# First chunk of a Mamba layer: order of loads, norms, bias sums and row fetches

## Chip, cores, metric

One core of one Trainium2 chip. The metric is device time in microseconds, the median of several executions. The kernel before was run three times: 5859.45, 5865.35 and 5869.25 us.

## The reference

The input is x, (4, 384, 64, 64) in float32. Two layers follow each other, each added to its input after a group norm. The first is a Mamba block over the 4096 tokens of each image; the second is a windowed attention with convolved values (outlook), which the change does not touch. The Mamba block, cut:

```python
xn = layernorm(group_norm(x)) * ln_w + ln_b              # per token, 384 channels
xb, z = split(xn @ in_proj_w.T)                          # 768 channels each
xc = silu(causal_conv4(xb) + conv_b)
dt, Bm, Cm = split(xc @ x_proj_w.T)                      # 24, 16, 16
dt = softplus(dt @ dt_w.T + dt_b)
h = exp(dt * A) * h + (dt * xc) * Bm                     # per channel 16 states, over the tokens
y = (h . Cm + xc * D) * silu(z)
out = y @ out_proj_w.T
```

## The kernel before, in words

Each image is cut along its tokens into 17 chunks of 241, so there are 68 chunks. A chunk goes through a front (norm, projections, convolution, dt, B and C), a scan and an end (gate, output projection). The scan of a chunk is cut into 12 units: a unit has two groups of 32 channels with 16 states, held as 128 partitions by eight rows of 242 in a tile h. For a unit, POOL and DVE multiply the rows of dt*x (dxr) with B into h (s_inputs, line 747, and s_inputs2, line 762), ACT makes the decays da = exp(dt*A) in eight activations (s_decay, 771), DVE scans twice (s_scan, 783), POOL multiplies h with C (s_outputs, 793) and PE sums over the states (s_sum, 798).

The rows of dt and dt*x must lie four times over the partitions. So the front stores dt (f_log, 477) and dt*x (f_dtx, 509) to DRAM, tensors dtd and dxd, with four DMAs for each store, and SP reads them back for two units at a time, again in four DMAs each: s_fetch (731) reads dxr from dxd, s_fetch_dt (740) reads dtr from dtd. f_xd (444) and f_spread (483) do the same for B and C through bcd.

Nothing is scheduled by a planner. Each engine runs what the program issues, in the order in which it issues it (class InOrder, whose line 53 is why all instructions stand under L53 in the profile; they are told apart by the names of their tiles). The tool that builds the program adds semaphore waits by the tiles that an instruction reads and writes, and reuses buffers by pool: the pool pmm has two PSUM buffers for nearly all matmul results of the front. All DMAs here are issued by SP, over eight semaphores in turn, so a DMA also waits for the eighth before it.

In the steady state a loop over steps s (line 949) issues the parts of up to six chunks by a written plan (line 605), with the scan of unit s, the inputs of units s + 1 and s + 2, and the outputs of unit s - 1. Ahead of it a straight piece of code (lines 886 to 946), the head, brings the first chunk to the end of its front and the second chunk to the end of its norm. In the loop's first steps the second chunk's projection (f_x, 358) is issued at step -1, and the rest of its front is caught up (catch_up, 677).

The head's steps that the change moves: loads (213 to 231 and f_load, 281); group-norm coefficients of the image (x_coeffs, 184); the norm over channels in seven parts (f_mean, f_center, f_square, f_var, f_root, f_pow, f_scale, lines 289 to 333), which run on PE, DVE, ACT, PE, ACT, ACT, DVE in that order; w_bias (247), which multiplies the projection's weights by the norm's bias in one-column matmuls into the tile pw, six blocks for each half of the weights' columns; w_scale (258), which copies those sums to bxz and scales the weights win by the norm's weight; w_taps (235), which writes the convolution's diagonal matrices cdiag on POOL; f_conv (379), f_silu (410), f_bc (434, tile ps_xd), f_dt (454, ps_dt), f_plog (504, ps_lg), f_z (400, tile zs).

Of the kernel before, what the change touches and what calls it, by code (L numbers as in the profile page):

```python
# [7 lines left out]
F32 = mybir.dt.float32  # L8
# [4 lines left out]
P = 128  # L13
C = 384
NCB = C // P
# [95 lines left out]
def mamba_layer(ctx, tc, x, w, x1, sc1, bi1, bi4, consts, early, behind):  # L111
# [40 lines left out]
    def load(name, shape, pool=wp):  # L152
        t = pool.tile(shape, F32, tag=name, name=name)
        sp.dma_start(t, w[name])
        return t
# [58 lines left out]
    for i in range(NCB * NX):  # L214
        x_stat(0, i, x_load(0, i))

    lnw = load("lnw", [P, NCB], wf)
    lnb = load("lnb", [P, NCB], wf)
    win = wf.tile([P, NCB, 2 * DI], F32, tag="win", name="win")
    sp.dma_start(win[:, :, :DI], w["win"][:, :, :DI])  # L220
    cw = load("cw", [P, NJ, KC], wf)
    cbias = load("cbias", [P, NJ], wf)
    wx = load("wx", [P, NJ, P], wf)
# [23 lines left out]
    def w_bias(j0, j1):  # L247
        for j in range(j0, j1):
            for cb in range(NCB):
                pe.matmul(  # L250
                    pw[:, j : j + 1],
                    win[:, cb, j * P : (j + 1) * P],
                    lnb[:, cb : cb + 1],
                    start=(cb == 0),
                    stop=(cb == NCB - 1),
                )

    def w_scale(half):
        js = slice(NJ * half, NJ * (half + 1))
        ve.tensor_copy(bxz[:, js], pw[:, js])  # L260
        for cb in range(NCB):
            part = win[:, cb, DI * half : DI * (half + 1)]
            ve.tensor_scalar(part, part, lnw[:, cb : cb + 1], None, ALU.mult)
# [17 lines left out]
    def f_load(c):  # L281
        c.xt = iof.tile([P, NCB, XT], F32, tag="xt", name="xt")
        sp.dma_start(
            c.xt[:, :, : c.n], x[c.b, :, c.t0 : c.t0 + c.n].rearrange("(p cb) l -> p cb l", cb=NCB)
        )
        if c.n < TM:
            gp.memset(c.xt[:, :, c.n : TM], 0.0)

    def f_mean(c):
        t = c.t  # L290
        c.sc, avs, c.bias = coeffs[c.b]
        c.ps = pmm.tile([P, 2, TM], F32, tag="mm", name="ps_ln")
        for cb in range(NCB):
            pe.matmul(c.ps[:, 0, :t], avs, c.xt[:, cb, :t], start=(cb == 0), stop=(cb == NCB - 1))

    def f_center(c, u=None):

        t = c.t
        c.u = front.tile([P, NCB, TM], F32, tag="u", name="u") if u is None else u
        ve.scalar_tensor_tensor(  # L300
            c.u[:, :, :t],
            c.xt[:, :, :t],
            c.sc,
            c.ps[:, 0:1, :t].to_broadcast([P, NCB, t]),
            ALU.mult,
            ALU.subtract,
        )

    def f_square(c, room=None):
        t, u = c.t, c.u  # L310
        if room is None and c is live.get(2):
            room = xo.rearrange("p cb r w -> p cb (r w)")[:, :, 2 * XT :]
        if room is None:
            room = front.tile([P, NJ, KC - 1 + TM], F32, tag="xb", name="sq")
        c.sq = room[:, :NCB, :TM]
        ae.activation(c.sq[:, :, :t], u[:, :, :t], AF.Square, bias=c.bias)

    def f_var(c):

        t = c.t  # L320
        c.ps = pmm.tile([P, 2, TM], F32, tag="mm", name="ps_var")
        for cb in range(NCB):
            pe.matmul(c.ps[:, 0, :t], avg, c.sq[:, cb, :t], start=(cb == 0), stop=(cb == NCB - 1))

    def f_root(c):
        v = c.ps[:, 0, : c.t]
        ae.activation(v, v, AF.Ln, bias=eps)

    def f_pow(c):
        v = c.ps[:, 0, : c.t]  # L330
        ae.activation(v, v, AF.Exp, scale=-0.5)
# [26 lines left out]
    def f_x(c, jj):  # L358
        t = c.t
        if jj == 0:  # L360
            c.xb = front.tile([P, NJ, KC - 1 + TM], F32, tag="xb", name="xb")
            if c.t0 == 0:
                ae.copy(c.xb[:, :, 0 : KC - 1], pad.unsqueeze(2).to_broadcast([P, NJ, KC - 1]))
            else:
                ae.copy(c.xb[:, :, 0 : KC - 1], halo[c.b])
        pp = project(c, jj)
        ae.copy(c.xb[:, 2 * jj : 2 * jj + 2, KC - 1 : KC - 1 + t], pp[:, :, :t])
        if jj == NJ // 2 - 1 and c.t0 + c.n < L:
            halo[c.b] = small.tile([P, NJ, KC - 1], F32, tag="halo", name="halo")
            ae.copy(halo[c.b], c.xb[:, :, t : t + KC - 1])  # L370
# [8 lines left out]
    def f_conv(c, jj):  # L379
        t = c.t  # L380
        if jj == 0:
            c.xc = []
        c.xc.append(cross.tile([P, 2, 1 + TM], F32, tag=f"xc{jj}", name="xc"))
        c.cv = pp = pmm.tile([P, 2, TM], F32, tag="mm", name="ps_cv")
        for h in range(2):
            j = 2 * jj + h
            for k in range(KC):
                pe.matmul(
                    pp[:, h, :t], cdiag[:, j, k, :], c.xb[:, j, k : k + t], start=(k == 0), stop=(k == KC - 1)
                )  # L390
        if jj < NJ // 2 - 1:
            conv_out(c, jj, AF.Identity)
        first_column(c, c.xc[jj], c.last.xc[jj] if c.ci else None)
# [491 lines left out]

    first, second, third = chunk(0), chunk(1), chunk(2)
    spare = xo.rearrange("p cb r w -> p cb (r w)")
    f_load(first)
    f_load(second)
    sp.dma_start(win[:, :, DI:], w["win"][:, :, DI:])  # L890
    ssum = load("ssum", [P, CG])
# [4 lines left out]
        norm_part(norms[0][1])  # L896
    w_taps(0, 2)
    f_mean(first)
    w_bias(0, 2)
    f_center(first)  # L900
    f_load(third)
    f_square(first)
    f_var(first)
    w_bias(2, 3)
    f_root(first)
    f_pow(first)
    w_bias(3, NJ)
    f_scale(first)
    w_scale(0)
    ve.tensor_scalar_mul(pad, bxz[:, :NJ], -1.0)  # L910
    w_taps(2, NJ)
    f_x(first, 0)
    f_mean(second)
    ve.reduce_sum(cws, cw, AX.X)
    ve.tensor_mul(cws, cws, bxz[:, :NJ])
    ve.tensor_add(cbias, cbias, cws)
    f_center(second, spare[:, :, :TM])
    f_x(first, 1)
    f_square(second, spare[:, :, XT:])
    f_conv(first, 0)  # L920
    f_var(second)
    f_root(second)
    f_pow(second)
    f_x(first, 2)
    f_scale(second)
    f_conv(first, 1)
    f_conv(first, 2)
    f_silu(first)
    w_bias(NJ, 2 * NJ)
    w_scale(1)  # L930
    f_bc(first)
    f_xd(first)
    f_spread(first)
    for jj in range(NJ // 2):
        f_dt(first, jj)
    f_b(first)
    for jj in range(NJ // 2):
        f_plog(first, jj)
        f_dtx(first, jj)
    f_log(first)  # L940
    ae.activation(aneg, aneg, AF.Exp)
    ve.tensor_scalar_mul(aneg, aneg, -1.0)
    for j in range(NJ):
        gp.tensor_scalar(ddiag[:, j, :], ident, dvec[:, j : j + 1], None, ALU.mult)
    for jj in range(NJ // 2):
# [2 lines left out]
    front_end = NU * (len(chunks) - 1) - 1  # L948
    for s in range(-4, NU * (len(chunks) + 2)):
        k, m = divmod(s, NU)  # L950
        if m % 2 == 0 and unit(s + 4) is not None:
            s_fetch(s + 4)
        if m % 2 == 0 and unit(s + 2) is not None:
            s_fetch_dt(s + 2)
        parts(s, EARLY)
        if m % 4 == 3 or s >= NU * len(chunks):
            norm_part(False)

        if (u := unit(s + 1)) is not None:
            s_inputs2(u)  # L960
        if (u := unit(s - 3)) is not None and not u.first and u.j % 2:
            s_gate(u)
        parts(s, READY)

        b, ci = chunks[k][:2] if 0 <= k < len(chunks) else (B, 0)
        if b + 1 < B:
            n, e = divmod(NU * ci + m - 3, NU // 2)
            if e == 0 and 0 < n <= NCB * NX:
                x_stat(b + 1, n - 1, pending.pop())
            if e == 1 and 0 <= n < NCB * NX:  # L970
                pending.append(x_load(b + 1, n))
            if e == 2 and n == NCB * NX:
                x_coeffs(b + 1)
        for i in range(2):
            if (u := unit(s)) is not None:
                s_scan(u, i)
            if i == 1:
                parts(s, SCAN)
            if (u := unit(s + 1)) is not None:
                if i == 0:  # L980
                    s_carry(u)
                s_decay(u, i)
            if i == 0 and (u := unit(s - 1)) is not None:
                s_save(u)
        if (u := unit(s - 1)) is not None:
            s_outputs(u)
        norm_part(True)
        parts(s, POOL)
        if (u := unit(s + 2)) is not None:
            s_inputs(u)  # L990
        if (u := unit(s - 2)) is not None and not u.first:
            s_sum(unit(s - 3), u)
        parts(s, MID)
        parts(s, LATE)
        if s == front_end:
            fronts.close()
        if s >= front_end:
            over = das[0] if s >= NU * len(chunks) - 1 else None
            behind(lambda: pmm.tile([P, 2, TM], F32, tag="mm", name="psv").rearrange("p a b -> p (a b)"), over)
# [592 lines left out]
```

## Time and profile before

| what | us |
|---|---|
| median of three executions | 5865.35 |
| profiled execution, its own time | 5861.92 |
| its span, first to last instruction | 5860.1 |
| busy: POOL, PE, DVE, ACT | 5392.2, 5295.0, 5241.6, 4848.9 |
| first projection of the first chunk starts (PE) | 45.54 |
| first store of dt*x is issued (SP) | 82.92 |
| first decay starts (ACT) | 101.48 |
| first scan starts (DVE) | 103.19 |
| first outputs of POOL start | 107.57 |

Times in the timeline are from the start of the span. A row of it merges equal instructions that follow each other: start, length of the whole row, engine, operation, written tile and read tiles, count; the bracket tells how long the engine was idle before the row and what ended that. A float32 matmul is shown as two passes, each with its weight load (PEld), so x12 is six matmuls. SPq is SP's queue of DMA issues; the row's length is that of issuing, not of landing.

### The profile page before, as it was taken

The page shows a single profiled execution, that of the slowest core. Times are in us where ns is not written, and L with a number is a line of the kernel's source. Part 1 is how long each engine was busy: PE and PEld are TensorE (multiplying, and loading weights), DVE is VectorE, ACT ScalarE, POOL GpSimd, SP SyncE. Part 2 cuts the span into 40 slices and gives each one's busy share as a digit, 9 for nine tenths or more (in the row PEclk, how much of TensorE's full clock was granted, in tenths as well). Part 3 has the DMA queues.
Part 4 walks back from the last instruction along what each step waited for, and adds up shares of the span by engine and source line. Part 5 has one row for each costly group of instructions (what it writes and reads, how often), then busy time and mean ns, then how long its engine had stood idle before and what let it go on. Part 6 is the DMA issues. An engine that isn't in the chain of part 4 may idle for free.

```text
span 5860.1 us, 126156 instructions
## 1 busy us (share of the span) xinstructions
PE 5295.0 (90%) x46114; PEld 3820.7 (65%) x46114; DVE 5241.6 (89%) x4269; ACT 4848.9 (83%) x13283; POOL 5392.2 (92%) x2045
## 2 busy tenths in 40 slices
PE   6888888888999999998999999999999995899999
PEld 5666666666666666666666666666666663666555
DVE  4999999999999999999999999999999997787444
ACT  4888888888888888888898888889889885677665
POOL 3999999999999999999999999999999998899433
PEclk9999999999999999999999999999999997999999
DMA  4555554445666666666666666656666655666444
GB/s 133 145 142 143 143 144 134 131 131 139 166 169 174 171 179 162 173 171 159 176 177 174 179 168 171 170 148 173 170 167 169 162 152 158 199 211 206 159 168 154
DMA packets 758875, 955.11 MB, mean 163 GB/s; under 512 B 211488, under 2 KB 660972, under 8 KB 758124
## 3 DMA queue, kind: packets, MB, share of 16 engines
q1 hardware_dynamic: 758252, 947.04, 58.7%
q8 instruction: 362, 5.93, 0.4%
q14 instruction: 261, 2.14, 0.1%
HBM read 720.92 MB, written 225.70 MB: 162 GB/s over the span
## 4 chain that ended last, share of the span: by engine, by line
ACT 36%; PE 25%; DVE 17%; DMA 5%; POOL 5%; SPq 4%; issue 4%; DVEq 0%; ACTq 0%; POOLq 0%
ACT da L53 20%; DVE h L53 14%; PE ps_in L53 4%; SPq L53 4%; POOL h L53 4%; PE ps_v L53 4%; PE y L53 3%; PE psv L53 3%; ACT L53 3%; PE ps_cv L53 2%; PE ps L53 2%; ACT zs L53 2%; PE pso L53 2%; ACT xc L53 2%; PE psa L53 2%
## 5 line engine op out<-in xcount | busy, mean ns | idle before, releaser
L53 DVE TENSOR_TENSOR_SCAN h<-da,h 128x968 f32<-128x968 f32 x1632 | 3453.9, 2158 | 151.6 <-POOL h L53 74.7
L53 POOL TENSOR_TENSOR h<-h,bc 128x1928 f32<-128x1928 f32 x816 | 3231.1, 3960 | 45.2 <-DVE h L53 41.3
L53 ACT ACTIVATE da<-dtr,alog 128x241 f32<-128x241 f32 x6528 | 2657.5, 455 | 370.0 <-DVE h L53 291.1
L53 POOL TENSOR_TENSOR h<-dxr,bc 128x964 f32<-128x964 f32 x816 | 1622.8, 1989 | 65.7 <-DMA dxr<-dxd 48.7
L53 PE MATMUL ps_in<-u,win 128*128 128x241 f32 x4824 | 1056.9, 370 | 37.2 <-ACT xb L53 26.4
L53 PEld LDWEIGHTS ps_in<-u,win 128*128 128x128 f32 x4824 | 903.7, 190 | 161.2 <-ACT xb L53 49.1
L53 DVE TENSOR_TENSOR h<-dxr,bp 128x964 f32<-128x964 f32 x816 | 928.7, 1138 | 10.5 <-DMA dxr<-dxd 9.2
L53 PE MATMUL y<-h,ssum 128*32 128x241 f32 x13056 | 782.9, 373 | 70.9 <-POOL h L53 70.7
L53 PE MATMUL ps_cv<-xb,cdiag 128*128 128x241 f32 x3264 | 718.1, 373 | 26.6 <-ACT zs L53 21.3
L53 PEld LDWEIGHTS ps_cv<-xb,cdiag 128*128 128x128 f32 x3264 | 606.3, 190 | 133.7 <-issue 34.0
L53 PEld LDWEIGHTS y<-h,ssum 128*32 128x32 f32 x13056 | 434.6, 111 | 343.6 <-POOL h L53 93.3
L53 POOL TENSOR_TENSOR bd<-ain,own 99x1188 f32<-99x1188 f32 x192 | 431.0, 2266 | 211.4 <-PE ps L53 196.9
L53 PE MATMUL ps_out<-zs,wout 128*128 128x241 f32 (+1 forms) x2448 | 563.8, 382 | 0.0
L53 ACT ACTIVATE bd<-ain,own 99x216 f32<-99x216 f32 (+1 forms) x1408 | 467.5, 420 | 113.1 <-PE ps L53 102.2
L53 PEld LDWEIGHTS ps_out<-zs,wout 128*128 128x128 f32 x2448 | 489.2, 200 | 43.2
L53 PE MATMUL ps_v<-wq,xo 128*32 128x384 f32 x4752 | 425.0, 489 | 32.4 <-ACT xr L53 29.8
L53 DVE TENSOR_TENSOR fold<-fold,ps 128x192 f32<-128x192 f32 (+1 forms) x768 | 210.3, 302 | 185.2 <-PE ps L53 171.8
L53 PE MATMUL ps_dt<-xd,wdt 128*128 128x241 f32 x816 | 227.1, 403 | 91.4 <-ACT xd L53 52.9
L53 PEld LDWEIGHTS ps_v<-wq,xo 128*32 128x32 f32 x4752 | 140.8, 110 | 240.5 <-issue 163.3
L53 PE MATMUL pso<-fold,wpr 128*128 128x256 f32 (+6 forms) x990 | 275.4, 425 | 3.7 <-DVE fold L53 3.3
L53 PE MATMUL ps<-bd,vin 99*32 99x99 f32 (+1 forms) x9216 | 228.2, 250 | 46.4 <-DVE fold L53 21.1
L53 PEld LDWEIGHTS ps<-bd,vin 99*32 99x32 f32 (+1 forms) x9216 | 200.5, 109 | 102.8 <-issue 44.8
(128 smaller groups left out, 5544.8 us busy)
## 6 DMA issues: line engine op xcount, KB each, us to landing
dxr<-dxd SPq DMA_DIRECT2D x1632, 120.5 KB
dtr<-dtd SPq DMA_DIRECT2D x1632, 120.5 KB
wq<-in_wv SPq DMA_DIRECT2D x297, 192.0 KB
dxd<-dtx SPq DMA_DIRECT2D x816, 60.2 KB
dtd<-dt SPq DMA_DIRECT2D x272, 180.8 KB
ve<-v SPq DMA_DIRECT2D x198, 192.0 KB
bc<-bcd SPq DMA_DIRECT2D x272, 120.5 KB
vin<-ve SPq DMA_DIRECT2D x66, 445.5 KB
```

Source lines behind the costliest of these rows:

```text
L53: made = self.tc.keep_in_program_order(issue(*args, **kwargs))
```

## The change

Four things are moved, and no arithmetic is added or dropped. The first chunk's x tile is read directly behind the x rows of the statistics, and the first half of win is loaded in three DMAs, ahead of lnw. The bias sums of the first half of the weights (w_bias) all stand ahead of the first chunk's variance. The second chunk's norm goes behind the first chunk's convolutions, and the end of it (f_var to f_scale) behind the stores of dt*x. The second half's bias sums and scaling go from ahead of f_bc to behind f_b. Of dt*x only the first third is stored before dt itself; then the first units' rows are fetched (s_fetch(0), s_fetch_dt(0), which the loop issued at steps -4 and -2), and the other two thirds are stored behind them.

```diff
--- before.py
+++ after.py
@@ -214,10 +214,13 @@
     for i in range(NCB * NX):
         x_stat(0, i, x_load(0, i))
 
-    lnw = load("lnw", [P, NCB], wf)
+    xt = iof.tile([P, NCB, XT], F32, tag="xt", name="xt")
+    sp.dma_start(xt[:, :, :TM], x[0, :, :TM].rearrange("(p cb) l -> p cb l", cb=NCB))
     lnb = load("lnb", [P, NCB], wf)
     win = wf.tile([P, NCB, 2 * DI], F32, tag="win", name="win")
-    sp.dma_start(win[:, :, :DI], w["win"][:, :, :DI])
+    for cb in range(NCB):
+        sp.dma_start(win[:, cb, :DI], w["win"][:, cb, :DI])
+    lnw = load("lnw", [P, NCB], wf)
     cw = load("cw", [P, NJ, KC], wf)
     cbias = load("cbias", [P, NJ], wf)
     wx = load("wx", [P, NJ, P], wf)
@@ -885,7 +888,7 @@
 
     first, second, third = chunk(0), chunk(1), chunk(2)
     spare = xo.rearrange("p cb r w -> p cb (r w)")
-    f_load(first)
+    first.xt = xt
     f_load(second)
     sp.dma_start(win[:, :, DI:], w["win"][:, :, DI:])
     ssum = load("ssum", [P, CG])
@@ -896,50 +899,54 @@
         norm_part(norms[0][1])
     w_taps(0, 2)
     f_mean(first)
-    w_bias(0, 2)
+    w_bias(0, 4)
     f_center(first)
     f_load(third)
     f_square(first)
+    w_bias(4, NJ)
+    w_scale(0)
     f_var(first)
-    w_bias(2, 3)
     f_root(first)
     f_pow(first)
-    w_bias(3, NJ)
     f_scale(first)
-    w_scale(0)
     ve.tensor_scalar_mul(pad, bxz[:, :NJ], -1.0)
     w_taps(2, NJ)
     f_x(first, 0)
-    f_mean(second)
     ve.reduce_sum(cws, cw, AX.X)
     ve.tensor_mul(cws, cws, bxz[:, :NJ])
     ve.tensor_add(cbias, cbias, cws)
+    f_x(first, 1)
+    f_conv(first, 0)
+    f_x(first, 2)
+    f_conv(first, 1)
+    f_mean(second)
+    f_conv(first, 2)
     f_center(second, spare[:, :, :TM])
-    f_x(first, 1)
+    f_silu(first)
     f_square(second, spare[:, :, XT:])
-    f_conv(first, 0)
-    f_var(second)
-    f_root(second)
-    f_pow(second)
-    f_x(first, 2)
-    f_scale(second)
-    f_conv(first, 1)
-    f_conv(first, 2)
-    f_silu(first)
-    w_bias(NJ, 2 * NJ)
-    w_scale(1)
     f_bc(first)
     f_xd(first)
     f_spread(first)
     for jj in range(NJ // 2):
         f_dt(first, jj)
     f_b(first)
-    for jj in range(NJ // 2):
-        f_plog(first, jj)
-        f_dtx(first, jj)
+    w_bias(NJ, 2 * NJ)
+    f_plog(first, 0)
+    f_dtx(first, 0)
+    f_plog(first, 1)
+    f_plog(first, 2)
     f_log(first)
+    s_fetch(0)
+    s_fetch_dt(0)
+    f_dtx(first, 1)
+    f_dtx(first, 2)
+    f_var(second)
+    f_root(second)
+    f_pow(second)
+    w_scale(1)
     ae.activation(aneg, aneg, AF.Exp)
     ve.tensor_scalar_mul(aneg, aneg, -1.0)
+    f_scale(second)
     for j in range(NJ):
         gp.tensor_scalar(ddiag[:, j, :], ident, dvec[:, j : j + 1], None, ALU.mult)
     for jj in range(NJ // 2):
@@ -948,9 +955,9 @@
     front_end = NU * (len(chunks) - 1) - 1
     for s in range(-4, NU * (len(chunks) + 2)):
         k, m = divmod(s, NU)
-        if m % 2 == 0 and unit(s + 4) is not None:
+        if m % 2 == 0 and s > -4 and unit(s + 4) is not None:
             s_fetch(s + 4)
-        if m % 2 == 0 and unit(s + 2) is not None:
+        if m % 2 == 0 and s > -2 and unit(s + 2) is not None:
             s_fetch_dt(s + 2)
         parts(s, EARLY)
         if m % 4 == 3 or s >= NU * len(chunks):
```

## Prediction

> **What bounds the kernel now.** I read the table of stretches first (busy time of each engine by stretch of the span; columns: us, then PE, PEld, DVE, ACT, POOL busy with instruction counts, granted clock, DMA share, GB/s).
>
> ```profile
> 100.00:140.00 40.00, 29.48 (x160) 24.72 (x160) 27.24 (x17) 30.66 (x80) 31.16 (x13) 0.91 0.30 83
> ...
> 200.00:1000.00 800.00, 692.63 (x4993) 531.75 (x4992) 781.07 (x523) 694.81 (x1910) 796.48 (x275) 0.94 0.53 140
> 1000.00:4700.00 3700.00, 3422.42 (x27625) 2480.89 (x27628) 3547.99 (x2353) 3265.85 (x8947) 3649.46 (x1282) 0.99 0.62 165
> ```
>
> From 200 to 4700 us POOL is busy 796.5 of 800 and 3649.5 of 3700 us: the loop is as long as POOL's work. The change touches nothing there. It touches what comes before the loop fills, so its worth is how much earlier the first units reach POOL. That is read from the timeline of the first 120 us, engine by engine (start, length, what; in brackets the idle time before and what ended it).
>
> ```profile
> 45.54 5.16 PE L53 MATMUL ps_in<-u,win 128*128 128x241 f32 x12 [0.88 <-DVE win L53]
> 51.76 2.61 PE L53 MATMUL ps_in<-u,win 128*128 128x241 f32 x12
> 67.64 4.56 PE L53 MATMUL pw<-lnb,win 128*128 128x1 f32 x36
> 72.07 5.17 PE L53 MATMUL ps_xd<-xc,wx 128*128 128x241 f32 x12
> 105.29 6.77 PE L53 MATMUL ps_in<-xo,win 128*128 128x241 f32 x24 [6.16 <-ACT xb L53]
> ```
>
> Twelve passes of 241 columns take 2.61 us at full clock and 5.16 at half. Behind 4.6 us of the one-column passes of pw (67.64) the granted clock falls to 0.50 (72 to 75 us), and ps_xd pays double.
>
> ```profile
> 82.92 6.00 SPq L53 DMA_DIRECT2D dxd<-dtx  x12
> 89.02 2.31 SPq L53 DMA_DIRECT2D dtd<-dt  x4
> 91.37 5.44 SPq L53 DMA_DIRECT2D dxr<-dxd  x8
> 96.85 2.03 SPq L53 DMA_DIRECT2D dtr<-dtd  x4
> ```
>
> ```profile
> 101.48 3.18 ACT L53 ACTIVATE da<-dtr,alog 128x241 f32<-128x241 f32 x8 [7.45 <-DMA dtr<-dtd]
> ...
> 109.66 0.56 ACT L53 COPY xb<-ps_in 128x482 f32<-128x482 f32 x1 [3.96 <-PE ps_in L53]
> ...
> 110.46 3.18 ACT L53 ACTIVATE da<-dtr,alog 128x241 f32<-128x241 f32 x8
> ```
>
> ```profile
> 103.19 4.24 DVE L53 TENSOR_TENSOR_SCAN h<-da,h 128x968 f32<-128x968 f32 x2 [4.43 <-ACT da L53]
> ```
>
> So the first decays (da) wait for the rows of dt, which SP fetches behind 24 other DMAs; unit 1's decays (110.46) wait for the second chunk's third projection on a PE that had gone idle and slow. From the scans of unit 1 on, ACT, DVE and POOL follow each other closely. Two dates therefore decide: the first da (101.48) and unit 1's (110.46).
>
> **The change part by part.**
>
> *Loads.* xt of the first chunk is issued behind the last x row (about 20.3 instead of 25.71). Today ps_ln starts at 32.02, released by that load; pb is done at 30.76. New start 30.6: 1.4 us earlier. The two added issues (win in three) and the shuffled small loads cost SP some 0.5 us each, in front of an idle stretch (30.97 to 35.88); cw and win have to be there at 29.8 and 33.2, and the trace's landings, 28.3 and 28.1 us, move by about 1 us. Nothing.
>
> *Bias sums ahead of the variance.* From ps_ln to the first projection today: 45.54 - 32.02 = 13.5 us. Now one chain: ps_ln 2.54, 36 pw passes (12 in 2.43, 24 in 5.12, so 7.5), ps_var 2.76, root and power 0.44 + 0.36, u's scaling 0.97, handovers 0.2: 14.8. The scaling of win hides behind ps_var. First projection at 30.6 + 14.8 = 45.4: the load's gain is spent here (-0.1).
>
> *Second chunk's norm behind the convolutions.* From the first projection to the end of the third convolution today 67.80 - 45.54 = 22.3 us; ps_var of the second chunk (1.2) leaves this stretch, ps_ln (1.3) stays. End at 66.4 (-1.4). Its Square (0.90 on ACT) now stands ahead of the copy of xd.
>
> *w_bias of the second half behind dt.* ps_xd follows the third convolution at once, at full clock: 66.3 + 2.6 = 69.0 (today 77.24). ACT: last xc 67.3, table load 1.28, Square 0.90, copies 0.2 + 0.36: xd at 70.0 instead of 77.68, **-7.7**. SP's bcd, bc, the three dt, three ps_lg and dt's logarithm shift alike.
>
> *dt and the rows ahead.* SP: first dtx store (4) from 82.92 - 7.7 = 75.2 to 77.2; dt's logarithm is done at 77.0, so its four stores run 77.3 to 79.6; dxr of unit 0 (half of 5.44) to 82.3. Two waits are added, each for the landing of what SP has just stored. The four dt stores, by the 4.6 us from dtr's first issue to da, are down at 82 to 82.6; dtr is issued then and lands at 82.6 + 4.6 = **87.2** (today 101.48). Behind these waits stand the stores of the second and third dtx, the rows of units 2 and 4 and dtr of unit 2. They run 84.6 to 95.5; unit 2's rows land near 93.4, POOL wants them by its first output, near 96; its dtr lands near 98, wanted at 101.5. Covered by 2 to 4 us, and each us beyond would cost one.
>
> *What is late next: z.* ACT's queue has the six zs copies ahead of the first da, and they wait for PE. PE: bp done at 81.43 - 7.7 = 73.7; pw 4.6, to 78.3; ps_var 1.4 to 2.8, to 79.7 or 81.0. The third dtx waits for the first one's landing (today 86.48), so 78.8 to 79.4, then bxz and the first third of win: 80.2. z starts at 80.2 to 81.0. Then six projections in a row (z three times, second chunk three times) at 4.88 for two (117.79 to 122.67) on full clock: 14.7, so 95.7 when the start is 81.0. Unit 1's da comes 0.8 to 0.9 behind (copy, halo): 96.7 + c. First da: z is done at 81.0 + 7.4, zs 0.9, carry 0.1: 89.4 + c; dtr (87.2) is earlier. Between the two, ACT needs 8 da (3.2) and two copies, to 93.3, just when PE needs its buffer.
>
> *c, the clock.* Real work stops at 73.7 for 4.6 us. In before it dropped 3.3 us behind such a stop (67.80 to 71.06) and rose 5.0, 5.8 and 3.3 us after work resumed (45.54, 72.07, 105.29). At 5 us after 78.3, PE is slow until 83: 2 us at half price behind 81.0, and up to 0.9 in pw. I take c = 1.3; bounds -0.9 (no drop, start at 80.2) and 14.7 + 3 (slow throughout), nearest the three rises.
>
> [...]
>
> *Sum.* First da 90.7 against 101.48: -10.8. Unit 1's da 98.0 against 110.46: **-12.5**. Unit 0's scan ends near 96.6; unit 1's gates everything behind: scan 1 at 99.7, POOL's second output at 104 (today 116.56). Nothing later is reordered, and POOL, DVE and ACT are all earlier by about the same, so the loop keeps it. 5861.9 - 12.5 = 5849.4 for the profiled execution (span 5860.1, 1.8 around it). The median shown, 5865.35, is 3.4 above that execution: **5853**.
>
> **Rivals.**
> - A: the rows bind after all. For: SP's chain has three landings in series, and today 3.6 us pass from the first dtx store's issue to its landing. If stores and fetches mixed take 2 us more each, first da is near 93 and unit 2's rows hold POOL: only the 7.7 us of xd remain. 5857.5. Chance 0.17.
> - B: the clock does not fall in pw. z at 80.2, c = -0.9, unit 1's da at 95.8: -14.7, 5850.7. For: the stop is 4.6 us, not much above 3.3. Chance 0.14.
> - C: given back. Chunk 1's dt path has its own gaps at 154 to 160 us (ACT idle 2.75, POOL 2.91). Were they bound to the head's DMAs and not to the steps, they would eat it: 5862 to 5865. Against: each of them ends on DVE or ACT work of the step before. 0.06.
> - D, slower: the clock stays low from pw through all six projections, as it did up to 50.6 us by the length of the passes (the clock's row reads 1.00 there, yet six passes take 2.76). pw 7.7, ps_var 2.8, six times 5.1: 73.7 + 41.1 + 0.9 = 115.7, 5.2 later than today: 5870.5. It decides once the slow clock costs 13 us over c = 1.3, that is some 27 us slow without a break. Against: at 105.29 it rose within 3.3 us of steady projections. 0.04.
>
> **Numbers.** Forecast 0.59, 5853, own spread 5850 to 5856. The executions shown spread by 5 us to each side. Eight in ten: 5846 (B and 5 us) to 5860 (A and 2.5). 0.2% is 11.7 us, about what a measurement of this kernel can tell from no change; the bound is 5853.6, just above the forecast. Faster: 0.41 of the forecast's 0.59, B's 0.14 and 0.02 of A: 0.57. Same: 0.18 + 0.15 + 0.06 + D's 0.01: 0.40. Slower 0.03.
>
> **What would show it.** ps_xd right behind ps_cv in 2.6 us; xd's copy near 70; dtr's last landing near 87 with ACT by then in front of zs; first da released by PE's ps_in through zs, not by dtr; unit 1's da near 98; the clock at 0.50 somewhere between 76 and 84. Wrong would be: da released by dtr, POOL's third input waiting for dxr past 96, or a head earlier by 12 us with a span that is not.

## The result, and the profile after

| | before | after |
|---|---|---|
| median, side by side, 15 runs each (us) | 5861.73 | **5850.84** |
| lowest and highest | 5857.36, 5869.85 | 5842.46, 5858.15 |
| profiled execution, its own time | 5861.92 | 5847.95 |
| its span | 5860.1 | 5846.2 |
| first projection of the first chunk (PE) | 45.54 | 45.75 |
| copy of xd starts (ACT) | 77.33 | 70.17 |
| first store of dt*x issued (SP) | 82.92 | 76.17 |
| first decay (ACT) | 101.48 | 92.11 |
| unit 1's first decay (ACT) | 110.46 | 99.48 |
| POOL's second output | 116.56 | 105.56 |

The ratio is 0.9982, with a 95% interval of 0.9975 to 0.9988: 10.9 us or 0.18% faster. The interval leaves out no change, and the bound of 0.2% that the prediction set lies inside it, so a gain above 0.2%, to which the prediction gave 0.57, is neither shown nor excluded. Unit 1's decays, the date that the prediction called decisive, come 11.0 us earlier.

First the table of stretches of the kernel after (columns as in the prediction):

```profile
100.00:140.00 40.00, 33.10 (x234) 25.39 (x232) 32.26 (x20) 34.62 (x91) 33.43 (x13) 0.96 0.29 80
200.00:1000.00 800.00, 692.06 (x5020) 531.82 (x5013) 782.72 (x527) 690.86 (x1907) 796.77 (x276) 0.95 0.53 142
```

The loop is what it was: POOL is busy 796.77 of 800 us. Only the stretch from 100 to 140 us is fuller on every engine, since the units come sooner. Now PE's timeline of the head:

```profile
45.75 7.79 PE L53 MATMUL ps_in<-u,win 128*128 128x241 f32 x24 [2.01 <-DVE pad L53]
...
66.83 2.61 PE L53 MATMUL ps_xd<-xc,wx 128*128 128x241 f32 x12
...
74.05 4.08 PE L53 MATMUL pw<-lnb,win 128*128 128x1 f32 x36
77.99 2.30 PE L53 MATMUL ps_var<-xo,avg 128*128 128x241 f32 x6
82.15 9.14 PE L53 MATMUL ps_in<-u,win 128*128 128x241 f32 x36 [1.86 <-DVE win L53]
```

ps_xd follows the convolution and takes 2.61 us instead of 5.17. The bias sums of the second half (pw) now lie behind bp, and z (the row at 82.15, three projections) takes 9.14 us; by the prediction's 14.7 for six it would take 7.35 on full clock. The table of stretches says why, in its eighth column, the granted clock:

```profile
78.50:85.30 6.80, 4.94 (x13) 3.68 (x12) 3.42 (x8) 0.98 (x3) 0.00 (x0) 0.50 0.75 184
```

SP's queue, by the time of issue:

```profile
76.17 2.87 SPq L53 DMA_DIRECT2D dxd<-dtx  x4
79.15 2.32 SPq L53 DMA_DIRECT2D dtd<-dt  x4
...
84.64 1.85 SPq L53 DMA_DIRECT2D dtr<-dtd  x4
...
90.51 5.00 SPq L53 DMA_DIRECT2D dxr<-dxd  x8
```

The rows of dt are asked for at 84.64 instead of 96.85; in the trace the last of them lands at 89.05. ACT's copy of xd in the kernel before, then ACT after, and then DVE after:

```profile
77.33 0.35 ACT L53 COPY xd<-ps_xd 56x241 f32<-56x241 f32 x1 [7.16 <-PE ps_xd L53]
```

```profile
70.17 0.35 ACT L53 COPY xd<-ps_xd 56x241 f32<-56x241 f32 x1
...
91.32 0.81 ACT L53 ACTIVATE zs<-ps_in,bxz 128x241 f32<-128x241 f32 x2 [1.63 <-PE ps_in L53]
...
92.11 3.17 ACT L53 ACTIVATE da<-dtr,alog 128x241 f32<-128x241 f32 x8
...
99.48 3.16 ACT L53 ACTIVATE da<-dtr,alog 128x241 f32<-128x241 f32 x8
```

```profile
80.83 0.66 DVE L53 TENSOR_TENSOR dtx<-ps_lg,xc 128x482 f32<-128x482 f32 x1 [4.99 <-ACT ps_var L53]
...
93.83 4.24 DVE L53 TENSOR_TENSOR_SCAN h<-da,h 128x968 f32<-128x968 f32 x2 [4.26 <-ACT da L53]
```

The first decays have no bracket: ACT goes from the last zs copy straight to them, and that copy waited for PE. Before, the same row had "7.45 <-DMA dtr<-dtd". The wait for the rows is gone, and z is what is late. The row at 80.83 is the third dt*x, one of two buffers' third user. The bracket names ACT's ps_var, which this product does not read; it is the store of the first one that must have landed, and its last part lands at 80.61. (In a second execution of this kernel the bracket reads "5.09 <-DMA dxd<-dtx".) Behind it stands the scaling of win, and behind that z.

Last POOL:

```profile
95.48 1.98 POOL L53 TENSOR_TENSOR h<-dxr,bc 128x964 f32<-128x964 f32 x1 [4.60 <-DMA dxr<-dxd]
98.20 3.94 POOL L53 TENSOR_TENSOR h<-h,bc 128x1928 f32<-128x1928 f32 x1 [0.74 <-DVE h L53]
```

Unit 2's rows do hold up POOL's third input (95.48), but POOL's first output then still waits 0.74 us for DVE: those rows are covered by 0.74 us. POOL's second output, before and then after, still waits for DVE, 11.0 us sooner:

```profile
116.56 3.95 POOL L53 TENSOR_TENSOR h<-h,bc 128x1928 f32<-128x1928 f32 x1 [3.12 <-DVE h L53]
```

```profile
105.56 3.95 POOL L53 TENSOR_TENSOR h<-h,bc 128x1928 f32<-128x1928 f32 x1 [1.49 <-DVE h L53]
```

### The profile page after: what moved, and what is told of

It is laid out like the page before. It is cut to its first block, busy times and chain, and to the rows that moved or that the text cites. A ratio compares the mean times of both kernels' runs of the same rounds, so it can differ in the third digit from the quotient of the medians.

```text
span 5846.2 us, 126163 instructions
## 1 busy us (share of the span) xinstructions
PE 5286.2 (90%) x46114; PEld 3817.1 (65%) x46114; DVE 5240.3 (90%) x4269; ACT 4832.4 (83%) x13283; POOL 5393.8 (92%) x2045
## 5 line engine op out<-in xcount | busy, mean ns | idle before, releaser
L53 PE MATMUL ps_in<-u,win 128*128 128x241 f32 x4824 | 1059.8, 371 | 43.2 <-ACT xb L53 30.6
```

Source lines behind the costliest of these rows:

```text
L53: made = self.tc.keep_in_program_order(issue(*args, **kwargs))
```

## Experiments

My theory: the loop passes the head's time on one to one; the head ends at the later of two dates, the landing of dtr and the projections on PE; after the change PE's z binds, and what it lost against the forecast is a late start (the wait for the first dt*x store) and a low clock. The rivals: the rows bind (A), or the gain is given back in the first chunks (C). Each group of kernels ran on one chip beside the kernel before: 5866.32 us (27 runs) for the first group, 5868.56 (one run) for the second, 5867.01 (33 runs) for the third.

### The two main parts, apart

The kernel before with the row queue alone (dt and the rows ahead of most of dt*x, and the loop's two conditions):

```diff
-    for jj in range(NJ // 2):
-        f_plog(first, jj)
-        f_dtx(first, jj)
+    f_plog(first, 0)
+    f_dtx(first, 0)
+    f_plog(first, 1)
+    f_plog(first, 2)
     f_log(first)
+    s_fetch(0)
+    s_fetch_dt(0)
+    f_dtx(first, 1)
+    f_dtx(first, 2)
```

> The kernel before with one part of the change alone: the first third of dt*x, then dt, then the first units' rows, then the rest of dt*x. Theory (two paths, rows and projections, meet at unit 1's decays): xd stays near 77.7, dt's rows land near 96 instead of 101.4, the first decay starts at 96.3; the third projection of the second chunk then waits for ACT's copy near 100.2, unit 1's decays start near 103.7 instead of 110.46: about -6.8 us in all, 5855. Rival (the row queue is what the gain is made of): nearly all of the changed kernel's 11 us, unit 1's decays below 101.

```profile
95.59 3.17 ACT L53 ACTIVATE da<-dtr,alog 128x241 f32<-128x241 f32 x8 [1.88 <-DMA dtr<-dtd]
```

Unit 1's decays at 102.94, 7.5 us earlier, where the theory had 103.7; 5861.84 us (11 runs), ratio 0.9991 (0.9982 to 1.0), so 4.5 us below before where 6.8 were expected.

The kernel after with that part undone (the diff above, backwards):

> The changed kernel with the row queue undone: all of dt*x is stored ahead of dt, and the first rows are fetched in the loop again. Theory: xd stays at 70.5, the rows land 7.1 us earlier than in the kernel before, near 94.3, and end the wait of the first decay; unit 1's decays start near 101.4 instead of 99.48. So this part is worth 2 us of the 11, and the kernel stays about 9 us under the one before, 5853. Rival (the row queue is what the gain is made of): the first decay is back near 101, and at most 4 us are left.

Measured: 5861.25 us (11 runs), ratio 0.9992 (0.9983 to 1.0001), and unit 1's decays at 105.26, 5.8 us later than with the part. The theory had put it at 2 us. On ACT and on PE:

```profile
95.43 3.16 ACT L53 ACTIVATE da<-dtr,alog 128x241 f32<-128x241 f32 x8 [3.85 <-DMA dtr<-dtd]
```

```profile
99.23 8.04 PE L53 MATMUL ps_in<-xo,win 128*128 128x241 f32 x24 [3.72 <-ACT xb L53]
```

The rows alone cost 3.3 us (95.43 against 92.11). But while ACT waits for them, it does not copy xb, so PE finds no free buffer and stands for 3.72 us; the clock is granted at 0.50 from 98.3 to 105.1, and two projections take 8.04 us instead of about 4.9. That is the other 2.5 us: in the kernel with the row queue alone PE stood for only 0.57 us, two projections took 5.15 us, and unit 1's decays came 7.35 us behind the first ones, as in the kernel after (7.37); here they come 9.83 us behind.

```profile
99.39 5.15 PE L53 MATMUL ps_in<-xo,win 128*128 128x241 f32 x24 [0.57 <-ACT xb L53]
```

The kernel before had the same pair, "7.45 <-DMA dtr" on ACT and 6.77 us for two projections at 105.29.

The kernel before with only the second half's bias sums moved:

```diff
-    w_bias(NJ, 2 * NJ)
-    w_scale(1)
     f_bc(first)
...
     f_b(first)
+    w_bias(NJ, 2 * NJ)
...
     f_log(first)
+    w_scale(1)
```

> The kernel before with one other part alone: the second half's bias sums go behind bp, their scaling behind the stores of dt*x. Theory: the sums of xd follow the convolution at once at full clock, xd is there near 70.8 instead of 77.7, the rows near 94.5, unit 1's decays near 101.5: -9 us, 5853, alone nearly as much as the whole change. Rival (the row queue is what the gain is made of): the z projections, now behind the one-column passes and on a slow clock, take back what xd won: less than 4 us.

Measured: unit 1's decays at 105.23, 5.2 us earlier and not 9; 5862.07 us (11 runs), ratio 0.9988 (0.998 to 0.9997). First decays at 96.31, released by dtr; PE stood 3.12 us for xb behind them, and two projections took 6.72 us. So each of the two parts alone leaves a wait: -7.5 with the rows, -5.2 with the bias sums, -11.0 with all four parts. I had expected the two to overlap far more. In time the intervals of these three kernels reach to no change or almost (1.0, 1.0001 and 0.9997), so how the gain divides is read from the dates.

### Does the loop pass the head's time on?

The kernel after, with ACT held by 21 copies of zs onto itself in front of the first decays:

```diff
     for jj in range(NJ // 2):
         f_z(first, jj)
+    for _ in range(21):
+        ae.copy(first.zs[:, :, 1:], first.zs[:, :, 1:])
```

> The changed kernel with 21 copies of the tile zs onto itself on ACT (1.41 us each by the row of its Silu, 29.6 us) right ahead of the first carry and decay. Theory (the head's time goes into the total one to one): +29 to +30 us against the changed kernel, about 5880, and the scans stay late by the same amount to the end of the loop. Rival C (waits behind the head take up part of it): less than +25 us, with a shift that shrinks along the loop.

```profile
93.32 29.95 ACT L53 COPY zs<-zs 128x1446 f32<-128x1446 f32 x21
```

```profile
127.08 7.59 PE L53 MATMUL ps_in<-xo,win 128*128 128x241 f32 x24 [29.76 <-ACT xb L53]
```

Held for 29.95 us, the first decays come 31.2 us later than in the kernel after, unit 1's 33.6 later (the clock again: two projections in 7.59 us), and the sixteenth output of POOL 34.2 later. The time: 5892.77 us (4 runs), ratio 1.0042 (1.0028 to 1.0055) to the kernel before, so 26.5 us slower than before and some 37 slower than after, where 29 to 30 were expected; 34.2 of them are there at the sixteenth output, and with four runs the interval is 8 us to each side. Nothing is given back: rival C falls for delays of this size.

### Who holds z

One run each, so only the dates in the head are read here.

The third dt*x in a place of its own, a part of the tile xo that lies free, so that it waits for no store:

```diff
-    def f_dtx(c, jj):
+    def f_dtx(c, jj, dtx=None):
...
-        dtx = front.tile([P, 2, TM], F32, tag="dtx", name="dtx", bufs=2)
+        if dtx is None:
+            dtx = front.tile([P, 2, TM], F32, tag="dtx", name="dtx", bufs=2)
...
-    f_dtx(first, 2)
+    f_dtx(first, 2, spare[:, :2, 2 * XT : 2 * XT + TM])
```

> The changed kernel with a place of its own for the third dt*x product of the first chunk, so that it does not wait for the first one's landing. Theory: DVE scales win as soon as the bias sums are done, z starts near 80.2 instead of 82.15; the clock is slow until about 85.3 all the same, so of 2 us about 1 is left: first decay near 91.1, unit 1's near 98.5. Rival (rows bind by then): first decay released by the rows of dt, unit 1's decays not before 99.

Measured: z starts at 80.26 instead of 82.15, the clock is low for some 3.4 us only by the lengths of the passes (ps_var in 2.19 us, z in 8.51), the first decays come at 89.91 and are released by dtr (after a wait of 0.18 us), unit 1's at 97.26: 2.2 us earlier, where 1 was expected. The wait was real, and right behind z lie the rows.

Full-width matmuls between the one-column passes of pw, into columns that nobody reads, to keep the clock up:

```diff
-    w_bias(NJ, 2 * NJ)
+    for j in range(NJ, 2 * NJ):
+        w_bias(j, j + 1)
+        pe.matmul(pw[:, 2 * NJ :], avg, second.sq[:, 0, 2 * NJ : TM], start=True, stop=True)
```

> The changed kernel with one more matmul of 229 columns (two passes, 0.43 us) behind each of the six blocks of the second half's bias sums; their results go to unused columns of pw. They add 2.6 us to PE between 74 and 82, where it now idles 1.86 us ahead of the z projections. Theory (the one-column passes let the clock fall, and that costs the z projections 1.5 us): no fall near 78, z in 7.7 us instead of 9.14, unit 1's decays near 98.0 instead of 99.48. Rival (the clock is not what holds z): the date stays within 0.3 us, or gets later by PE's added work.

```profile
79.26 1.11 PE L53 MATMUL pw<-xo,avg 128*128 128x229 f32 x2
```

This expectation failed. Two such passes took 0.63 us at first (73.70) and 1.11 here: by the lengths of the passes the clock fell all the same, near 76.5, and stayed low to about 86.7. Unit 1's decays came at 102.25, 2.8 us later than in the kernel after and 1.3 later than in its second profile (100.98). What share of wide passes goes with a low clock is read off further down.

The bias sums and the variance of the first chunk in their old order (w_bias in pieces behind f_var and f_pow, w_scale behind f_scale):

> The changed kernel with the first half's bias sums back where they were, around the first chunk's variance; x is still read directly behind the statistics' rows. Theory: the sums of 4.6 us again lie beside ACT's and DVE's part of the norm, the first projection starts near 44.4 instead of 45.75, and all dates of the head follow: xd 68.9, unit 1's decays near 98.2. [...]

The first projection starts at 44.87 (0.9 earlier, though ps_ln starts 0.45 later in this execution: from ps_ln on it is 13.5 us instead of 14.9) and xd at 68.63 (1.5 earlier), but unit 1's decays at 99.34, only 0.1 earlier. By the lengths of the passes the clock stayed low for 10.2 us instead of 6.8, and z took 10.44 us. So that part of the change costs some 1.5 us at xd, and here the clock hid it: against the second profile of the kernel after, whose clock was low for 10.2 us too, unit 1's decays are 1.6 us earlier.

The second chunk's norm back among the first chunk's convolutions (f_mean to f_scale at their old places):

> The changed kernel with the second chunk's norm back among the first chunk's projections and convolutions. Theory: 1.2 us of variance passes come back ahead of xd, the Square of 0.9 leaves ACT's queue ahead of it: xd at 70.8. Behind the bias sums PE then has no real pass until z starts near 82.7, the clock falls and is slow until 86 or later: unit 1's decays 1 to 2.5 us later than 99.48. Rival (the norm's place is worth its passes alone): 0.5 to 0.7 us later.

```profile
82.09 10.30 PE L53 MATMUL ps_in<-u,win 128*128 128x241 f32 x36 [3.20 <-DVE win L53]
```

Unit 1's decays at 100.57, 1.1 later, at the lower end of the expectation, but for another reason. The convolutions end at 67.7 instead of 67.0; yet the Square no longer stands ahead of the copy of xd on ACT, and xd starts at 70.28, where the kernel after has 70.17. What the part wins on PE it gives back on ACT. z starts at 82.09, as in the kernel after. The 1.1 us lie in z, 10.30 us instead of 9.14: with ps_var gone from behind pw, PE stood still there for 3.20 us, and the clock was low for 10.2 us by the lengths of the passes. But that the norm's place is the cause is not shown. The kernel after, with ps_var in its place, had the same z in its second profile, and unit 1's decays at 100.98:

```profile
82.50 10.30 PE L53 MATMUL ps_in<-u,win 128*128 128x241 f32 x36 [1.06 <-DVE win L53]
```

What this part is worth at unit 1's decays stays open.

### A better head, and its worth

Four kernels on one chip, 11 runs each. The kernel after once more:

> The changed kernel once more, to stand beside the next three on one chip. Theory: first decays 92.1 us released by PE through the zs copies, unit 1's decays 99.5, 11 us ahead of before; median 9 to 13 us below before's.

The first decays were released by PE through zs, as expected, but came at 93.63, and unit 1's at 100.98: 1.5 us later than in the first profile, with the clock low for 10.2 us from 77.8 on, by the lengths of the passes (ps_var in 2.76 us, z in 10.30).

The place for the third dt*x, timed:

> The changed kernel with a place of its own for the third dtx, now timed. Theory (the wait for the first store's landing holds z, and the rows bind next): first decays 89.9 us, released by dtr; unit 1's decays 97.3; median 2 us below the changed kernel's, 13 below before's. Rival (the head's time is not passed on below some date, because POOL waits for unit 2's rows): POOL's outputs of unit 2 no more than 1 us earlier and the median within 1 us of the changed kernel's.

The same with the first chunk's old order of bias sums and variance, and the second chunk's Square behind the copy of xd:

```diff
-    f_square(second, spare[:, :, XT:])
     f_bc(first)
     f_xd(first)
+    f_square(second, spare[:, :, XT:])
...
-    w_bias(0, 4)
+    w_bias(0, 2)
...
-    w_bias(4, NJ)
-    w_scale(0)
     f_var(first)
+    w_bias(2, 3)
...
+    w_bias(3, NJ)
     f_scale(first)
+    w_scale(0)
```

> The changed kernel with that place, with the bias sums and the variance of the first chunk in the old order, and with the second chunk's Square behind the copy of xd on ACT. Theory: xd near 68.0 us (1.5 earlier by the first projection, 0.7 by the Square); first decays, bound by the rows, 87.5 to 88; unit 1's decays 95 to 96.5, so 1 to 2 us below the version with the place alone. Rival (the clock eats it): with an earlier stop the clock is slow for 6.8 us or more in front of z, z's nine projections' worth takes 10 us, unit 1's decays 97 or later and the median no lower.

The place, and the second chunk's projections ahead of the first chunk's z:

```diff
-            if s == -1 and when == POOL:
-                for jj in range(NJ // 2):
-                    f_x(second, jj)
...
     for jj in range(NJ // 2):
-        f_z(first, jj)
+        f_x(second, jj)
...
         parts(s, MID)
+        for jj in range(NJ // 2 if s == 0 else 0):
+            f_z(first, jj)
```

> The changed kernel with the place for the third dtx, and with the second chunk's three projections issued ahead of the first chunk's three of z, which go behind the middle parts of the loop's step 0. Theory: unit 1's decays no longer wait for the projections and start right behind unit 0's, near 95 to 96 us; but scan 1 then waits for DVE (scan 0 near 92 to 97, and what follows it), near 99, as in the version with the place alone; median within 1 us of that one. Rival (the projections alone hold unit 1): scan 1 at 97 or earlier and the median 2 us or more below it.

The dates of the profiled executions and the medians, all less those of the kernel before (101.48, 110.46 and 206.51 us, and the median beside it). The last two columns are what is to be compared:

| kernel | first decay | unit 1's decay | POOL's 16th output | median |
|---|---|---|---|---|
| after | -9.4 | -11.0 | -10.1 | -10.9 |
| after, again | -7.9 | -9.5 | -8.8 | -11.5 |
| row queue alone | -5.9 | -7.5 | -6.9 | -4.5 |
| after without row queue | -6.1 | -5.2 | -3.5 | -5.1 |
| second bias sums alone | -5.2 | -5.2 | -5.5 | -4.3 |
| after, ACT held | +21.8 | +22.6 | +24.1 | +26.5 |
| place of its own | -12.7 | -14.3 | -11.3 | -12.4 |
| place, old bias order, Square | -14.5 | -16.2 | -14.9 | -15.3 |
| place, z behind | -7.9 | -12.9 | -5.1 | -3.3 |

The ratios of the last group: after again 0.9979 (0.9971 to 0.9988) at 5855.50 us, place 0.9981 (0.9972 to 0.9989) at 5854.64, the combined one 0.9978 (0.9969 to 0.9987) at 5851.75, z behind 0.9993 (0.9984 to 1.0002) at 5863.67. Over a range of 40 us the median follows POOL's sixteenth output within 3 us, which is what such an interval (5 us to each side) allows. That is the theory of the loop, shown for the medians. Single spans do not follow as closely: the combined kernel's profile was 14.9 us ahead of before's at the sixteenth output and 5.3 at its end.

The place of its own had unit 1's decays 4.8 us ahead of the kernel after beside it (96.17 against 100.98), but POOL's sixteenth output only 2.5 us ahead. Of the 4.8 us 1.0 is not the edit's, since xd starts at 69.46 here and at 70.42 there. DVE, ACT and PE of its profile:

```profile
75.28 0.66 DVE L53 TENSOR_TENSOR xo<-ps_lg,xc 128x482 f32<-128x482 f32 x1
```

```profile
88.82 3.17 ACT L53 ACTIVATE da<-dtr,alog 128x241 f32<-128x241 f32 x8
```

```profile
79.65 8.11 PE L53 MATMUL ps_in<-u,win 128*128 128x241 f32 x36
...
115.79 3.11 PE L53 MATMUL y<-h,ssum 128*32 128x241 f32 x32
...
128.43 3.39 PE L53 MATMUL ps_dt<-xd,wdt 128*128 128x241 f32 x8 [2.47 <-ACT xd L53]
```

The third dt*x follows the second at 75.28 (80.83 before that edit), z starts at 79.65, and ACT has its first decays at 88.82, just behind the landing of dtr's last row (88.72). Against before, POOL's third output is 14.3 us earlier, its sixth 12.6 and its eighth 11.3. The loss lies in the last two lines. The clock is granted at 0.50 from 115.0 to 118.4, and the 32 passes of the sums y take 3.11 us; it is at 0.50 again from 128.7 to 132.1, and the eight passes of ps_dt take 3.39. In the first profile of the same kernel both took their short time, 1.82 and 1.90 us, and nothing was lost (13.2 us at unit 1's decays, 13.5 at the sixteenth output):

```profile
116.49 1.82 PE L53 MATMUL y<-h,ssum 128*32 128x241 f32 x32
...
127.86 1.90 PE L53 MATMUL ps_dt<-xd,wdt 128*128 128x241 f32 x8 [2.47 <-ACT xd L53]
```

The kernel after had ps_dt slow at 130.08, 3.36 us at a clock of 0.50, and lost 0.9 us by it. So the expected 2 us in the median were not found (0.9, inside the interval). The rival for this kernel, that POOL waits for unit 2's rows, does not explain it: its outputs of unit 2 came 4.5 us earlier than in the kernel after beside it. Rival C is half right: not the steps of the loop, but the clock's falls in the first chunks take up to 3 us back, differently in each profile.

The combined kernel has the best head: xd at 67.81, first decays 86.95, unit 1's 94.31, below the 95 to 96.5 expected. In front of z and within it its clock was at 0.50 for one stretch of 3.4 us only (76.1 to 79.5), so its rival (the clock eats it) failed here. The rows do not bind the first decays, as I had expected (dtr's last row landed at 86.64); they are level with z at the first scan:

```profile
88.66 4.24 DVE L53 TENSOR_TENSOR_SCAN h<-da,h 128x968 f32<-128x968 f32 x2 [1.76 <-POOL h L53]
```

The bracket names POOL's inputs, which had waited for dxr and ended at 88.62. But the scan starts 1.71 us behind the first decays, in the kernel after 1.72 us, so ACT's decays alone would have held it as long. This kernel has the lowest median measured beside the kernel after, 3.8 us below it; their intervals overlap, so only the head's 6.7 us (94.31 against 100.98) are shown, not the gain in time.

z behind the projections lost. My expectation looked at scan 1 alone, which came at 100.54 and not at 99. What was overlooked lies behind it, on PE, DVE and POOL:

```profile
102.02 4.13 PE L53 MATMUL ps_in<-u,win 128*128 128x241 f32 x12 [4.43 <-ACT zs L53]
```

```profile
109.85 0.97 DVE L53 SCALAR_TENSOR_TENSOR u<-xt,sc,ps_ln 128x723 f32<-128x723 f32 x1 [5.08 <-PE ps_ln L53]
```

```profile
116.17 3.96 POOL L53 TENSOR_TENSOR h<-h,bc 128x1928 f32<-128x1928 f32 x1 [4.75 <-DVE h L53]
```

z's third projection needs a buffer that ACT's zs copies free, and those stand behind unit 1's decays; the third chunk's ps_ln on PE stands behind z, DVE's u behind ps_ln, and unit 2's scan behind u. A step moved behind the critical one blocked the next unit on three queues.

## Why the prediction held, point by point

- **The bound, and the loop.** Right. POOL is busy as before, and time won in the head is passed on; shown over eight kernels besides before, one of them twice, and in both directions.
- **Loads, first bias sums.** ps_ln starts at 30.89 (forecast 30.6) and the first projection at 45.75 (45.4): the load's gain is spent there, as said. In the old order it was 44.87. The landing of cw moved by 1.9 us and not by 1, and POOL waited 0.18 us for it, off the path. No run changes the loads alone.
- **Norm behind the convolutions.** The third convolution ends at 67.0 (66.4), by the 0.35 us carried on and 0.2 more. At xd the part is worth 0.1 us, as PE's gain and ACT's Square cancel; in the forecast both stood too.
- **Second half's bias sums.** ps_xd in 2.61 us, at full clock. The copy of xd ends at 70.5, against 70.0 forecast.
- **Rows ahead.** Right in direction, late by 2 us: the first store issue 76.17 (forecast 75.2), dtr's issue 84.64 (82.6), its landing 89.05 (87.2). 0.5 us come from xd, 0.4 from a pause of SP's queue ahead of the first store (its product was done at 75.26, the issue before it at 75.66; what held SP until 76.17 the trace does not show), and 0.9 from the first stores, whose four issues took 2.87 us instead of 2, one of them 1.58. It cost nothing, because z was later still: 3 us of cover for dtr, 0.7 for unit 2's rows where I had counted 2 to 4. Rival A did not happen, but stood close: POOL's third input waited for dxr until 95.48, and past 96 was the sign of being wrong.
- **z is what is late next.** Right: the first decays are released by PE through zs. The start was mis-sized: 82.15 instead of 81.0, since the first store's landing came 2 us later than the 78.8 I had put it at, with that same long issue. The version with its own place starts at 79.65 and 80.26, inside or below my 80.2 to 81.0.
- **c, the clock.** 1.3 forecast; measured by z's 9.14 us against 7.35 it is 1.8. The fall came where it was forecast; its size differs between executions: the same code took 10.30 in its second profile.
- **The sum.** First decays -9.4 instead of -10.8, unit 1's -11.0 instead of -12.5. The 1.5 us are the two mis-sized terms: 1.15 from z's start and about 0.5 from the clock. The time came out 2.2 us below 5853 nonetheless, because the kernel before, run beside it, had its median at 5861.73 and not at 5865.35, from which I had started: two errors, 1.5 us up and 3.6 us down, that met by luck.
- **The rivals.** B (the clock does not fall in pw) is refuted in every trace, where it fell within pw or at most 0.5 us behind it, D (it stays low through all six projections) too: 3.4 to 10.2 us. C by the held ACT, up to the 1 to 3 us named above.

What I had not seen in the profile of before: its two dates were one. Its wait for dtr also stopped PE, through xb's buffer, and so the low clock at 105.29 (0.50 from 101.8 to 108.6, 6.77 us for 24 passes) belonged to that wait. That is why unit 1's decays gained 1.6 us more than the first ones.

## What to carry to other kernels

Where a loop is filled by one engine, price an edit ahead of it by the date at which its second unit starts, not the first, and look for who is released behind it: with the rows gone, z bound; with z freed, the rows bound again by 0.2 us, and in the combined kernel the two were level. An engine that waits for a transfer also holds the buffers that another engine needs, and on TensorE the stops of 3.12, 3.72 and 6.16 us behind such a wait were paid a second time as a low clock (24 passes in 6.72, 8.04 and 6.77 us), where a stop of 0.57 us was not (5.15 us). A step that is moved behind the critical one still stands in three queues: ask for each what is behind it there.

## What the runs showed of the hardware

In the traces of the kernels before and after the granted clock is on record from 50.6 and 51.2 us on. It reads 1.00 or 0.50, and each change in these records lies 3.41 us or a whole multiple of it behind the one before (62 and 57 low stretches). The first low stretch within or behind the second half's pw is 6.8 us long in both (71.1 to 77.9 and 78.5 to 85.3), and 3.4 us in the place of its own, timed (77.5 to 80.9), and in the combined kernel (76.1 to 79.5). In the other ten profiles, read from the lengths of the passes, it is near 3.4, 6.8 or 10.2 us.

I cut the time around the fall into pieces of 3.41 us, counted from the fall, and took the share of each that full-width passes filled. In the kernel after, the two pieces ahead of those in the table have 0.67 and 0.76, at a clock of 1.00. In the kernel before, where pw stands ahead of xd, the piece before the fall has 0.05, and the low stretch 0.71 and 0.85. Farther on the share alone does not decide the fall: behind a piece of 0.48 the clock fell in the place of its own, timed (111.6 to 115.0), and did not in the kernel before (125.7 to 129.1). The length of the low stretch is not the same from one execution to the next: three profiles with the same code up to z (the kernel after twice, and with ACT held) had 6.8, 10.2 and 10.2 us. From the end of the wide passes ahead of pw to the fall it took 2.1 to 4.4 us (the kernel with wide passes between pw's left out).

| kernel | share in the piece before the fall | shares in the low stretch | z, three projections (us) |
|---|---|---|---|
| after | 0.14 | 0.54, 0.92 | 9.14 |
| after, again | 0.03 | 0.73, 0.69, 1.00 | 10.30 |
| place of its own, timed | 0.06 | 1.00 | 8.11 |
| place, old bias order, Square | 0.13 | 1.00 | 8.36 |
| wide passes between pw's | 0.61 | 0.52, 0.73, 1.00 | 8.8, with a gap of 0.66 |

In the kernel after, 36 one-column passes filled PE's row for 4.08 us, from 74.05 on, and the clock fell all the same, at 78.5. In the three profiles in which z followed ps_var without a stop (the place of its own twice, and the combined kernel) the low stretch was near 3.4 us long; in the eight with a stop of 1.06 to 3.55 us in front of the projections, 6.8 or 10.2, also in the one of them that has the place of its own (z behind, a stop of 2.22 us). That the stop is the cause is my estimate; no run changes it alone. Unit 1's decays in the two profiles of the place of its own are 2.2 and 4.8 us ahead of the kernel after's in its two. More than half of that is z's earlier start (1.9 and 2.9 us, of which 1.0 in the second pair was there at xd), and the rest z's shorter run (0.6 and 2.2).

What stays open: why single issues of SP take 1.58 us among others of 0.3 to 1.0, and what moves single profiles against each other in the loop (the shift of the kernel after against before is 10.1 us at the sixteenth output and 13.9 at the end of those two spans, that of the combined kernel 14.9 and 5.3). The mean granted clock does not tell the two apart (0.975 and 0.976).
